# Two graph-attention layers on one core: the second layer's aggregates 1 to 4 split once more by Strassen

## The chip, the cores and the metric

The kernel runs on one core of a Trainium2 chip. Its engines are TensorE (matrix products, with a separate stream of weight loads), VectorE and ScalarE (elementwise work, and the only readers of PSUM, where TensorE writes), GpSimd (elementwise work in SBUF; it also issues the stores) and SyncE, which issues the loads. The metric is the device time of the program in microseconds, as the median of several runs.

## The reference, cut to what matters

There are 2708 nodes with 1024 features and an adjacency matrix of zeros and ones. Each of the two layers is a residual: x plus a graph attention of relu(layernorm(x)).

```python
# layer 0
h = relu(layernorm(x))
scores = where(adj > 0, relu((h @ Wf + bf) @ (h @ Wg + bg).T), NEG)
x = x + softmax(scores, axis=1) @ (h @ W + bW)
# layer 1
h = relu(layernorm(x))
hw = h @ W1
scores = where(adj > 0, leaky_relu(hw @ a1 + (hw @ a2).T), NEG)
x = x + relu(softmax(scores, axis=1) @ hw)
```

The kernel computes attention @ (h @ W) as (attention @ h) @ W. In layer 1 the scores need only two numbers per node, and the large products are attention @ h, called the aggregate, and the one with W, called the projection. All of it is float32.

## The kernel before, in words

**Tiling.** The 2708 rows are cut into 20 full tiles of 128 rows, one tile of 128 more (`MONO`) and one of 20 (`TINY`). The columns of the attention matrix, which are the output rows, are cut into five panels of 576, 576, 532, 512 and 512 (`width`, line 89). The full tiles go in ten pairs (`pairs`, line 109); ha and hb are the rows of a pair's two tiles.

**One Strassen level (Winograd's form, 7 products for 8).** An aggregate has three dimensions: the 1024 features, in two halves of 512 (4 column blocks of 128 each), the rows in pairs, where the two tiles of a pair are the two halves, and the panel's columns in two halves of width h. The left operand is made of the rows of h; its seven combinations M1 to M7 are stored in DRAM by `pair_h` (line 309; `rows_h` and `sums_h` in layer 0) and loaded again as `hc`. The right operand is made of the exponentials, called `P` in layer 1 (22 tiles per panel). `aggregate` (line 841) makes the right-hand sums T1, `second` and `fourth` and calls `accumulate` (line 603). There each of the seven half-wide products takes 10 pairs x 4 column blocks into four PSUM banks, in the order M1, M5, M2, M6, M3, M7, M4. The banks x, y, z and v are evicted by VectorE (ScalarE for M1 and M2). M6's banks go on to M7, M5's to M3, M1's to M2.

**Rows left over.** `MONO` and `TINY` don't take part in the splitting. `left_over` (line 877) adds them into the open banks of M2, M3 and M4, and into banks of its own in the middle of M7 (`into_m15`): one load `hl`, 8 instructions of 128 rows (line 883) and 8 of 20 rows that use a quarter of the array each (line 887).

**Scaling.** `inverse_sums` (line 814) makes the inverse sums of the softmax; the result gT is multiplied by them, mostly by GpSimd (`scale`, line 931), the last quarter by VectorE (line 939).

**What sets the order.** The Tile framework plans all instructions together by their place in the program and by its own estimates, so an engine may run one ahead of its place when its inputs are ready. Loads on SyncE's queue are pinned to program order by `load` (line 137). GpSimd's DMAs, stores and fetches alike, are not. Work for VectorE and ScalarE that has to fit between matmuls stands in a list, `later`, with an estimated time for each item. `behind(us)` (line 198) is called between groups of matmuls and issues items up to a credit:

```python
credit[0] = min(credit[0] + us, 2 * us)
while later and credit[0] > 0 and (psum_free or not later[0][3]) and (not later[0][4] or later[0][4]()):
    credit[0] -= one()
```

In the second layer's aggregates the rate is 4.0 after every third pair. The exponentials of the next panel are such items (`weights1`, line 1460, 24 items of 2.1 us). They are put in the list by a hook of `then`: `take_shifts` after M3 (it empties the list, takes column maxima with five transposes and makes the shifts) and `take_weights` after M7. `exps_until` (line 830) forces what isn't done when it is needed: half of the exponentials at the start of the aggregate, the rest after M5.

**Buffers.** There are 54 slots of 576 floats a partition (`slot`), 12 stream buffers of 1024 floats (`stream`; `hc`, `w` and the scores' operands are in these), two gT tiles and 8 PSUM banks.

**The scores loop of layer 0** (`scores`, line 1115) has already a form that the change takes over: for each pair, seven small products with accumulators X, Y and Z, in the order M1 X, M6 Z, M5 Y, M2 X, M7 Z, M3 Y and M4 Z. The last is delayed until after the next pair's first, so that VectorE has time to read Z.

Of the kernel before, what the change touches and what calls it, by code (L numbers as in the profile page):

```python
# [8 lines left out]
FP = mybir.dt.float32  # L9
# [48 lines left out]
def kernel(  # L58
# [69 lines left out]
    def stream(name, shape=(P, D), dt=FP):  # L128
        return strm.tile(list(shape), dt, tag="strm", name=name)
# [7 lines left out]
    def load(o, i):  # L137
        for a, b in in_16(o, i):
            tc.keep_in_program_order(nc.sync.dma_start(a, b))

    def store(o, i):
        for a, b in in_16(o, i):
            nc.gpsimd.dma_start(a, b)  # L143
# [10 lines left out]
    groups = [[q, q + 1] for q in range(0, NQ, 2)]  # L154
    group_of = {q: (i, j) for i, g in enumerate(groups) for j, q in enumerate(g)}
    assert sorted(group_of) == list(range(NQ))
    hg_d = [[dram.tile([P, 7, len(g), W], FP, name=f"hg{l}_d{i}") for i, g in enumerate(groups)] for l in range(2)]
    hsl_d = dram.tile([P, 2, NH, P], FP, name="hsl_d")
    hgl_d = [dram.tile([P, 2, W + P], FP, name=f"hgl{l}_d") for l in range(2)]
    md_d = dram.tile([P, 7, NH, W], FP, name="md_d")  # L160
    wt_d = [dram.tile([P, 4, NH, W], FP, name=f"wt{l}_d") for l in range(2)]
    mk_d = [dram.tile([P, NQ + 1, 2, width[p]], BF, name=f"mk_d{p}") for p in range(NP)]
# [17 lines left out]
        (nc.vector.tensor_copy if flip[0] else nc.scalar.copy)(o, i)  # L180


    later, credit = [], [0.0]
    ahead = [5]

    def put(us, go, fetch=None, takes_psum=False, ready=None):
        later.append([us, fetch, go, takes_psum, ready])

    def one():
        for it in later[:ahead[0]]:  # L190
            if it[1]:
                it[1]()
                it[1] = None
        us, _, go = later.pop(0)[:3]
        go()
        return us

    def behind(us, psum_free=False):
        credit[0] = min(credit[0] + us, 2 * us)
        while later and credit[0] > 0 and (psum_free or not later[0][3]) and (not later[0][4] or later[0][4]()):  # L200
            credit[0] -= one()

    def flush():
        while later:
# [96 lines left out]
    def left_h(l, hm, ht):  # L301

        for e in range(2):
            store(hgl_d[l][:, e, :W], hm[e])
            for d in range(NH):
                g = slice(B32 * d, B32 * (d + 1))
                store(hgl_d[l][g, e, W:], ht[e][g, d * P:(d + 1) * P])

    def pair_h(l, q, ha, hb):

        n = P
        on = nc.vector
        if q >= NQ - F // 2:
            s1, s2, s3, s4 = (slot(f"g{i}")[:, :W] for i in range(4))
            i, j = group_of[q]
            for m, h in ((M1, ha[0]), (M2, hb[0]), (M4, hb[1])):
                store(hg_d[l][i][:n, m, j], h)
            on.tensor_tensor(s1, ha[1], hb[1], OP.add)
            on.tensor_tensor(s2, s1, ha[0], OP.subtract)
            for m, h in ((M5, s1), (M6, s2)):  # L320
                store(hg_d[l][i][:n, m, j], h)

            def rest():
                on.tensor_tensor(s4, hb[0], s2, OP.subtract)
                on.tensor_tensor(s3, ha[0], ha[1], OP.subtract)
                for m, h in ((M3, s4), (M7, s3)):
                    store(hg_d[l][i][:n, m, j], h)
            return rest
        g1, g2 = stream("g1", (P, 2, W)), stream("g2", (P, 2, W))
        s1, s2, s3, s4 = g1[:n, 0], g1[:n, 1], g2[:n, 0], g2[:n, 1]  # L330
        on.tensor_tensor(s1, ha[1], hb[1], OP.add)
        on.tensor_tensor(s2, s1, ha[0], OP.subtract)
        on.tensor_tensor(s3, ha[0], ha[1], OP.subtract)
        on.tensor_tensor(s4, hb[0], s2, OP.subtract)
        i, j = group_of[q]
        for m, h in ((M1, ha[0]), (M2, hb[0]), (M4, hb[1])):
            store(hg_d[l][i][:n, m, j], h)
        store(hg_d[l][i][:n, M5:M6 + 1, j], g1[:n])
        store(hg_d[l][i][:n, M7:M3 + 1, j], g2[:n])

    def rows_h(q, ha, hb):

        i, j = group_of[q]
        for m, h in ((M1, ha[0]), (M5, ha[1]), (M2, hb[0]), (M4, hb[1])):
            store(hg_d[0][i][:, m, j], h)

    summed = [0]

    def sums_h():

        def fetch(q, two):
            i, j = group_of[q]
            for m in (M1, M2):
                two.append(stream("hr", (P, 2, W)))
                load(two[-1], hg_d[0][i][:, m:m + 2, j])

        def first(q, two):
            (a0, a1), (b0, b1) = ((t[:, 0], t[:, 1]) for t in two)
            add(b1, a1, b1)
            sub(a1, a0, a1)  # L360

        def second(q, two):
            (a0, a1), (b0, b1) = ((t[:, 0], t[:, 1]) for t in two)
            sub(a0, b1, a0)
            sub(b0, b0, a0)
            i, j = group_of[q]
            store(hg_d[0][i][:, M6:M7 + 1, j], two[0])
            store(hg_d[0][i][:, M3, j], b0)
            store(hg_d[0][i][:, M5, j], b1)
            summed[0] += 1  # L370
        for q in range(NQ):
            two = []
            put(1.4, lambda q=q, two=two: first(q, two), lambda q=q, two=two: fetch(q, two))
            put(1.4, lambda q=q, two=two: second(q, two))

    u = consts.tile([P, NC], FP, name="u")
    v = consts.tile([P, NC], FP, name="v")
# [463 lines left out]
    def aggregate(l, p, S, sm, then={}, rate=3.0):  # L841
# [28 lines left out]
        def left(m, q, d):  # L870
            i, j = group_of[q]
            if (m, i) not in hc:
                hc[m, i] = stream("hc", (P, 2, W))
                load(hc[m, i], hg_d[l][i][:, m])
            return hc[m, i][:, j, d * P:(d + 1) * P]

        def left_over(ps, e, s, start=False):


            two = stream("hl", (P, W + P))  # L880
            load(two, hgl_d[l][:, e])
            for d in range(NH):
                nc.tensor.matmul(ps[d], two[:, d * P:(d + 1) * P], S[MONO][:, s], start=start, stop=False,
                                 skip_group_check=True)
            for d in range(NH):
                g = slice(B32 * d, B32 * d + NY)
                nc.tensor.matmul(ps[d], two[g, W:], S[TINY][g, s], start=False, stop=start, skip_group_check=True)

        def into_m15():
            ps = [bank(f"gw{d}")[:, :h] for d in range(NH)]  # L890
# [40 lines left out]
        def scale():  # L931
            for e, s, k in ((0, slice(0, w), w), (1, hi, h)):
# [4 lines left out]
                   by_k=True, more={M2: lambda ps: left_over(ps, 0, lo), M3: lambda ps: left_over(ps, 0, hi),  # L937
                                    M4: lambda ps: left_over(ps, 1, lo), (M7, NQ // 2): into_m15})
        nc.vector.tensor_tensor(of(1, lo), of(1, lo), by(lo, h), OP.mult)
        return [t.rearrange("p (c i) -> p c i", c=NH) for t in G]  # L940

    w_in = [w0, w1]
# [166 lines left out]
    def put_max(p, q):  # L1109
        for k in range(2):  # L1110
            mk = []
            put(0.7, lambda k=k, mk=mk: raise_max(p, q, k, mk[0][:, :width[p]]),
                lambda k=k, mk=mk: mk.append(load_mask(p, q, k)))
# [164 lines left out]
        nc.vector.scalar_tensor_tensor(c, f1, ALPHA, m, op0=OP.mult, op1=OP.subtract)  # L1278
        return z, c, m

    done_rows, first_mask, raise_later = {}, {}, []

    def rows_done(t, xt):

# [13 lines left out]
        if panel_of[t] == NP - 1:  # L1298
            done_rows[t] = row_halves("h_last")
            normalize(xt, done_rows[t])  # L1300
            if whole and q == NQ - 1:
                tc.keep_in_program_order(nc.scalar.activation(stats.tile([P, 1], FP, name="warm"), eps, AF.Exp))
            raise_it = lambda: raise_max(0, q, k, first_mask[t][:, :width[0]])
            if not whole:
                dots(1)
                raise_later.append(raise_it)
                put(1.6, lambda: dots(0))
            else:
                raise_later.pop()()
                dots(1)  # L1310
                raise_it()
                put(1.6, lambda: dots(0))
                rest = []
                make = lambda: rest.append(pair_h(1, q, *(done_rows[s] for s in pairs[q])))
                if q == NQ - 1:
                    got["zm"] = shifts1(0, make)
                else:
                    make()
                rest[0]()
                for p in range(1, NP):  # L1320
                    put_max(p, q)
            return

        def met():
# [8 lines left out]
        if whole and q == LEFT:  # L1333
            put(0.0, lambda: left_h(1, *(done_rows[s] for s in mine)))
            put(0.0, met)
        elif whole:
            put(2.7, lambda: pair_h(1, q, *(done_rows[s] for s in pairs[q])))
            put(0.0, met)

    def halves_of_tiny(name):  # L1340
        t = slot(name)[:, :2 * P].rearrange("p (e j) -> p e j", e=2)
# [194 lines left out]
    def take_shifts(p):  # L1536
        flush()
        got["zm"] = shifts1(p)
# [5 lines left out]
    for p in range(NP):  # L1544
        S, sm = got["P"]
        then = {}
        if p + 1 < NP:
            then = {M3: lambda p=p: take_shifts(p + 1), M7: lambda p=p: take_weights(p + 1)}
        g = aggregate(1, p, S, sm, then, rate=4.0)
        project(1, p, g, finish1(p), by_pair=(p == NP - 1), rate=1.7)  # L1550


# [27 lines left out]
```

## Time and profile before

| | |
|---|---|
| median of 3 runs | 3132.92 us (3130.36 to 3140.10) |
| profiled execution: span, first to last instruction | 3135.8 us |
| profiled execution: time outside the span | not given by the page |
| TensorE matmul busy | 3053.1 us, 97% |
| weight loads busy | 2266.1 us, 72% |
| VectorE busy | 1835.6 us, 59% |
| ScalarE and GpSimd busy | 450.3 us and 427.3 us, 14% each |
| DMA | 666.04 MB, mean 212 GB/s |
| mean granted TensorE clock | 0.989 |

The second layer's aggregates start at 2157.27 us (panel 0), 2357.07, 2569.05, 2760.31 and 2941.69, and the projection follows each. The aggregates of panels 1 to 4 take 150, 138, 133 and 132 us. The profile comes as a page and as answers of the trace. A row of the timeline has a start in us, a duration, the engine, the line of the kernel, the operation, what it writes and reads, the shape and how many. A row of groups has the busy time and the mean duration in ns, then the engine's idle time before them and what ended it. Line 45 is that of a helper which issues every operation of VectorE and ScalarE, so these are told apart by their tiles. An f32 matmul of the program is two MATMUL instructions with two weight loads: the 40 matmuls of a half-wide product stand as x80.

### The profile page before, as it was taken

How to read it: one execution, taken by the hardware profiler on the slowest of the kernel's cores; microseconds unless marked ns; L12 is line 12 of the kernel's file. 1: busy time of each engine (PE TensorE's matmuls, PEld its weight loads, DVE VectorE, ACT ScalarE, POOL GpSimd, SP SyncE). 2: the span in 40 equal slices, each digit the busy share in tenths (PEclk: the TensorE clock that was granted, in tenths of full speed). 3: DMA queues.
4: the chain of work that ended last, by engine and by line, in shares of the span. 5: the costliest groups of instructions: out<-in, count | busy, mean ns of one | idle time of the engine just before them, and what ended most of it. 6: DMA issues, size and time to landing. Idle time of an engine off the chain costs nothing.

```text
span 3135.8 us, 36310 instructions
## 1 busy us (share of the span) xinstructions
PE 3053.1 (97%) x12694; PEld 2266.1 (72%) x12694; DVE 1835.6 (59%) x3767; ACT 450.3 (14%) x785; POOL 427.3 (14%) x654
## 2 busy tenths in 40 slices
PE   8998999899999999999999999998999999999998
PEld 4576777657877588886888885875757758678684
DVE  5766693776741686426973377758573571745612
ACT  3420020010200101101020002103131130311200
POOL 1421101310002110023000101021010020120202
PEclk9999999999999999999999999998999999999999
DMA  6989967988546796468955678597655565565655
GB/s 220 294 252 248 292 247 253 301 275 230 175 136 156 222 247 223 149 153 253 284 180 160 171 214 245 191 293 250 200 179 175 158 200 158 171 197 172 219 169 181
DMA packets 386278, 666.04 MB, mean 212 GB/s; under 512 B 171744, under 2 KB 212224, under 8 KB 386096
## 3 DMA queue, kind: packets, MB, share of 16 engines
q1 hardware_dynamic: 341936, 536.96, 56.9%
q0 software_dynamic: 44160, 126.76, 12.6%
q8 instruction: 101, 1.65, 0.2%
q14 instruction: 81, 0.66, 0.1%
HBM read 548.26 MB, written 115.30 MB: 212 GB/s over the span
## 4 chain that ended last, share of the span: by engine, by line
PE 81%; issue 6%; DVE 6%; DMA 5%; SPq 1%; POOL 1%; ACT 0%; POOLq 0%; DVEq 0%; ACTq 0%
PE gz L617 11%; PE gx L617 11%; PE gy L617 10%; PE sz L1140 6%; PE pz L1029 5%; PE gv L617 5%; PE sx L1140 4%; PE sy L1140 4%; PE px L1029 4%; PE py L1029 4%; PE M_ps L530 3%; PE qz L617 2%; PE qx L617 2%; PE qy L617 2%; DVE junk L45 1%
## 5 line engine op out<-in xcount | busy, mean ns | idle before, releaser
L1140 PE MATMUL sz<-B,As 128*128 128x288 f32 (+2 forms) x1200 | 295.9, 396 | 12.1 <-DVE st L45 7.9
L1140 PEld LDWEIGHTS sz<-B,As 128*128 128x128 f32 x1200 | 229.4, 192 | 63.1 <-DVE st L45 11.8
L933 POOL TENSOR_TENSOR gT<-gT,rr 128x2304 f32<-128x2304 f32 (+5 forms) x20 | 73.0, 3648 | 1081.4 <-DVE rr L45 979.3
L1140 PE MATMUL sx<-B,As 128*128 128x288 f32 (+2 forms) x800 | 201.5, 395 | 11.2 <-DMA As<-hs_d 9.1
L1140 PE MATMUL sy<-B,As 128*128 128x288 f32 (+2 forms) x800 | 199.3, 392 | 0.0
L617 PE MATMUL gz<-Sa,hc 128*128 128x288 f32 (+2 forms) x800 | 190.3, 399 | 5.9 <-DMA hc<-hg_d 5.9
L617 PE MATMUL gx<-P,hc 128*128 128x288 f32 (+2 forms) x800 | 187.0, 394 | 0.1
L617 PE MATMUL gz<-P,hc 128*128 128x288 f32 (+2 forms) x800 | 185.5, 392 | 0.0
L1140 PEld LDWEIGHTS sx<-B,As 128*128 128x128 f32 x800 | 152.5, 191 | 45.2 <-DMA As<-hs_d 10.1
L617 PE MATMUL gy<-T,hc 128*128 128x288 f32 (+2 forms) x800 | 184.2, 391 | 0.0
L617 PEld LDWEIGHTS gz<-Sa,hc 128*128 128x128 f32 x800 | 154.6, 194 | 40.0 <-DMA hc<-hg_d 6.4
L617 PEld LDWEIGHTS gx<-P,hc 128*128 128x128 f32 x800 | 152.4, 191 | 34.2 <-issue 3.7
L1140 PEld LDWEIGHTS sy<-B,As 128*128 128x128 f32 x800 | 152.3, 191 | 30.8
L617 PEld LDWEIGHTS gz<-P,hc 128*128 128x128 f32 x800 | 151.3, 190 | 31.6 <-issue 1.8
L617 PEld LDWEIGHTS gy<-T,hc 128*128 128x128 f32 x800 | 152.0, 190 | 30.5
L1029 PE MATMUL pz<-w,ps 128*128 128x512 f32 x320 | 142.1, 594 | 0.8 <-DVE pt L45 0.8
L1029 PE MATMUL py<-w,ps 128*128 128x512 f32 x320 | 141.9, 593 | 0.0
L1029 PE MATMUL px<-w,gT 128*128 128x512 f32 x320 | 141.0, 593 | 0.0
L143 POOL DMA_DIRECT2D out_dram<-x_res x180 | 89.2, 502 | 269.7 <-DVE x_res L45 264.5
L1029 PEld LDWEIGHTS pz<-w,ps 128*128 128x128 f32 x320 | 60.2, 190 | 77.1 <-issue 71.0
L1029 PEld LDWEIGHTS py<-w,ps 128*128 128x128 f32 x320 | 60.6, 190 | 75.5 <-issue 73.1
L530 PE MATMUL M_ps<-wgT,wfT 128*128 128x512 f32 x256 | 112.9, 597 | 1.6 <-ACT hsT L45 1.6
(319 smaller groups left out, 4894.9 us busy)
## 6 DMA issues: line engine op xcount, KB each, us to landing
hc<-hg_d SPq DMA_DIRECT2D x350, 512.0 KB, 3.7
As<-hs_d SPq DMA_DIRECT2D x150, 512.0 KB, 5.2
w<-wt_d SPq DMA_DIRECT2D x96, 512.0 KB, 4.9
w<-in_L_gnn_W_dram SPq DMA_DIRECT2D x72, 512.0 KB, 4.8
md<-md_d SPq DMA_DIRECT2D x56, 512.0 KB, 5.7
adj_i<-in_adj_dram SPq DMA_DIRECT2D x200, 128.0 KB, 5.2
hs_d<-hsT POOLq DMA_DIRECT2D x40, 512.0 KB, 7.2
As<-hs_d SPq DMA_DIRECT2D x50, 256.0 KB, 4.8
```

The costliest lines, as they stand in the source:

```text
L45: i = f(*a, **k)
L143: nc.gpsimd.dma_start(a, b)
L530: nc.tensor.matmul(ps, wfT[a][c // NH][:, c % NH, :], wgT[b][c], start=(c == 0), stop=(c == NC - 1))
L617: nc.tensor.matmul(ps[d], left(m, k, d), right(m, k), start=(start and k == 0), stop=(k == K - 1), skip_group_check=True)
L933: nc.gpsimd.tensor_tensor(of(e, s), of(e, s), by(s, k), OP.mult)
L1029: nc.tensor.matmul(ps, left[i][m][:, k, :], w_[k], start=(start and k == 0), stop=(k == NH - 1), skip_group_check=True)
L1140: nc.tensor.matmul(ps[:n, :h], lefts[q][:, i % 2, c, :n], B[m][c // 2][:, c % 2, :h], start=(start and c == 0), stop=(c == NH - 1), skip_g ...
```

## The change

Layer 0 and the second layer's panel 0 keep one level of Strassen. In panels 1 to 4, M1 and M5 stay half-wide, and each of M2, M6, M7, M3 and M4 (`BY_QUARTERS`) is split once more into seven small products. The second level takes as halves: the two pairs of a group of four tiles (5 groups, `NK`), two of the four column blocks, and a half of h (`hb`: 144, 133, 128 and 128 columns). A small product is then 5 groups x 2 column blocks, and lies in one PSUM bank.

- The left combinations of the layer's rows are all in one DRAM tile `hr_d`, in 1 KB pieces, ordered so that the groups of four tiles are neighbours. Of each split product, four more combinations per group are made by `put_quarters`: a fetch by GpSimd's queue, four adds of 256 columns, a store to `hs2_d`. These 25 items stand in a second list `lazy`, which `behind` serves when `later` is empty; `quarters_until` forces the rest.
- The right combinations (`quarter_sums`) are four subtractions of `hb` columns a group, 20 for each split product, issued during the product before.
- A split product loads nine stream buffers: one of four groups for each small product, and two that hold the fifth group for all of them.
- The results of the small products are added together in `V` and then into gT's quarters (`into_place`). The left-over rows go into the open banks X, Y, Z and a fourth, U; those of the (1,1) quarter go into four banks of their own (`corner`).
- In panels 1 to 3 `take_shifts` follows M7 and `take_weights` follows M3, as the order of products is now M1, M5, M2, M6, M7, M3, M4. The rate between small products is 1.2.

```diff
+    hr_d = dram.tile([P, 7, 2, 2, NK, WH], FP, name="hr_d")
+    hs2_d = dram.tile([P, 7, 4, NK, WH], FP, name="hs2_d")
...
-            store(hg_d[l][i][:n, m, j], h)
-        store(hg_d[l][i][:n, M5:M6 + 1, j], g1[:n])
+            store(rows_at(m, q), as_blocks(h))
+        store(rows_at(slice(M5, M6 + 1), q), as_blocks(g1[:n]))
...
+        while not later and lazy and credit[0] > 0:
+            credit[0] -= one(lazy)
...
+    BY_QUARTERS = (M2, M6, M7, M3, M4)
+    def put_quarters(m, k):
+        two = []
+        def fetch():
+            two.append(stream("hq", (P, 4, WH)))
+            nc.gpsimd.dma_start(two[0], hr_d[:, m, :, :, k].rearrange("p h f c -> p (h f) c"))
+        def go():
+            a11, a12, a21, a22 = (two[0][:, i] for i in range(4))
+            add(a22, a21, a22)
+            sub(a21, a11, a21)
+            sub(a11, a22, a11)
+            sub(a12, a12, a11)
+            store(hs2_d[:, m, :, k], two[0])
+            made_quarters[m] = made_quarters.get(m, 0) + 1
+        put(1.7, go, fetch, to=lazy)
...
+    def aggregate_quartered(p, S, sm, then={}, rate=3.0, fine=1.2):
...
+        def quarter_sums(m):
+            for k in range(NK):
+                r11, r12, r21, r22 = (part_of(m, k, i) for i in ((0, 0), (0, 1), (1, 0), (1, 1)))
+                four = slot("quarter", (P, 4, WX // 4))
+                t = {n: four[:, i, :hb] for i, n in enumerate((M5, M6, M7, M4))}
+                sub(t[M5], r12, r11)
+                sub(t[M6], r22, t[M5])
+                sub(t[M7], r22, r12)
+                sub(t[M4], r21, t[M6])
+                sums[m, k] = t
...
+        def product(m, n, ps, start):
+            quarters_until(m)
+            if (m, 0) not in lasts:
+                for i, of in enumerate((hr_d[:, m, :, :, NK - 1].rearrange("p h f c -> p (h f) c"), hs2_d[:, m, :, NK - 1])):
+                    lasts[m, i] = stream("hl2", (P, 4, WH))
+                    load(lasts[m, i], of)
+            t = stream("hc2", (P, NK - 1, WH))
...
+            load(t, hr_d[:, m, i // 2, i % 2, :NK - 1] if raw else hs2_d[:, m, i, :NK - 1])
+            last = lasts[m, int(not raw)][:, i]
+            for k in range(NK):
+                for d in range(2):
+                    lhs = t[:, k] if k < NK - 1 else last
+                    nc.tensor.matmul(ps[:, d], lhs[:, d * P:(d + 1) * P], inner_right(m, n, k),
+                                     start=(start and k == 0 and d == 0), stop=(k == NK - 1), skip_group_check=True)
+            behind(fine)
...
+        accumulate(left, operand, NQ, h, (M1, M5), then,
+                   {M1: first_product, M5: lambda d, ps: add(quad(0, hi)[:, d], ps, quad(0, lo)[:, d])}, "g",
+                   {M5: second}, rate=rate, by_k=True, more={(M5, NQ // 2): first_sums})
...
+        place = {M2: [(0, lo)], M6: [(0, hi), (1, lo)], M7: [(1, hi), (1, lo)], M3: [(0, hi)], M4: [(1, lo)]}
...
+        before_next = {M2: lambda: (fourth(), quarter_sums(M6)), M6: lambda: quarter_sums(M7),
+                       M7: lambda: quarter_sums(M3), M3: lambda: quarter_sums(M4)}
+        left_out = None
+        for m in BY_QUARTERS:
+            V = in_pairs("V")
...
+            X = bank2("gx")
+            product(m, M1, X, True)
+            nc.scalar.copy(c21, X)
+            if left_out:
+                left_out()
+            Z = bank2("gz")
+            product(m, M6, Z, True)
+            add(c12, Z, c21)
+            Y = bank2("gy")
+            product(m, M5, Y, True)
+            add(c22, Y, c21)
+            if m == M7:
+                corner()
+            if m in before_next:
+                before_next[m]()
+            product(m, M2, X, False)
+            if m not in more_of:
+                nc.scalar.copy(c11, X)
+            product(m, M7, Z, False)
+            add(c22, Z, c22)
+            product(m, M3, Y, False)
+            if m in more_of:
+                U = bank2("gu")
+                left_over({(0, 0): X, (0, 1): Y, (1, 0): Z, (1, 1): U}, *more_of[m], [(1, 1)])
+                nc.scalar.copy(c11, X)
+            add(c12, Y, c12)
+            if m in more_of:
+                add(c22, U, c22)
+            into_place(m, V, 0)
+
+            def left_out(m=m, V=V, Z=Z, c21=c21):
+                product(m, M4, Z, False)
+                add(c21, Z, c21)
+                into_place(m, V, 1)
+                if m == M3:
+                    scale()
...
-            then = {M3: lambda p=p: take_shifts(p + 1), M7: lambda p=p: take_weights(p + 1)}
-        g = aggregate(1, p, S, sm, then, rate=4.0)
+            then = dict(zip((M7, M3) if p else (M3, M7), (lambda p=p: take_shifts(p + 1), lambda p=p: take_weights(p + 1))))
+        g = aggregate_quartered(p, S, sm, then, rate=4.0) if p else aggregate(1, p, S, sm, then, rate=4.0)
```

## The prediction

> **What bounds the kernel now.** I read four things in order: the page's busy table, the chain that ended last, the engines by stage in the second layer, and TensorE's timeline inside one aggregate.
>
> The page's table of busy time, and its chain (shares of the span):
>
> ```profile
> PE 3053.1 (97%) x12694; PEld 2266.1 (72%) x12694; DVE 1835.6 (59%) x3767; ACT 450.3 (14%) x785; POOL 427.3 (14%) x654
> ...
> PE 81%; issue 6%; DVE 6%; DMA 5%; SPq 1%; POOL 1%; ACT 0%; POOLq 0%; DVEq 0%; ACTq 0%
> ```
>
> TensorE works nearly all the time and the chain is TensorE's. Busy time by stretch (us, then PE, PEld, DVE, ACT, POOL, clock, DMA share, GB/s), over panel 1's aggregate, and over three stretches of panel 0's:
>
> ```profile
> 2357.00:2507.00 150.00, 150.00 (x643) 115.53 (x642) 63.44 (x122) 20.98 (x38) 11.60 (x10) 1.00 0.53 162
> ```
> ```profile
> 2220.00:2239.00 19.00, 19.00 (x80) 14.89 (x79) 5.57 (x12) 0.37 (x1) 0.00 (x0) 1.00 0.45 129
> 2239.00:2262.00 23.00, 23.00 (x101) 17.56 (x100) 2.23 (x5) 0.00 (x0) 0.00 (x0) 1.00 0.61 186
> 2262.00:2286.00 24.00, 24.00 (x110) 18.27 (x109) 14.50 (x28) 0.42 (x2) 5.10 (x2) 1.00 0.46 144
> ```
>
> In the aggregates that change, TensorE is never idle, VectorE is idle for over half, and DMA moves 162 GB/s. So a matmul cycle saved here shortens the end, as long as the other engines keep up. The chain in order of time gives one half-wide product (80 instructions: 10 pairs of row tiles x 4 column blocks, each f32 matmul being two instructions) in panels 1, 2 and 3; panel 4 equals 3:
>
> ```profile
> 2376.63 19.40 PE gy L617 x80
> ...
> 2587.15 17.93 PE gy L617 x80
> ...
> 2777.74 17.27 PE gy L617 x80
> ```
>
> Per instruction that is 242.5, 224.1 and 215.9 ns for 288, 266 and 256 columns: 0.833 ns a column plus about 2.5 ns.
>
> **What the Trainium skill says.** (1) "TensorE: Matmul & The Clock Gate", Part 1, section "Wait — 56ns, not 53.3ns?": warm matmuls start N/2.4 GHz + about 2.5 ns apart. The trace agrees on the constant; f32 costs two cycles a column, in each of the two instructions. The same section says that without hardware decoding the sequencer spends about 62 ns a matmul; the slow loads and matmuls here can't show that. (2) The same page, Part 2, "Step-by-step: what each phase is for": the next tile's weights load while this one's matmul runs. The trace agrees (below). (3) "DMA: Bandwidth & Descriptors", Specifications: full rate from 512 B a piece, fabric 435 GB/s. The trace reached 405 GB/s over 40 us.
>
> **The change, part by part.** *Matmuls.* A split product has 7 small products x 5 k x 2 column blocks x 2 instructions = 140 of half the width, for 80 of the whole. At 144, 133 and 128 columns the fit gives 122.5, 113.3 and 109.2 ns. What the trace of before lacks is a 128-column f32 matmul with its own full weight load, whose record lasts 190 ns. Ends: 109.2 (load hidden) and 190 (loads never overlap). TensorE's matmuls, then its loads, near 62 us:
>
> ```profile
> 62.52 1.91 PE L399 MATMUL h_ps<-ident,x 128*128 128x128 f32 x16
> 64.26 1.02 PE L530 MATMUL M_ps<-wgT,wfT 128*128 128x512 f32 x2
> ```
> ```profile
> 62.41 1.78 PEld L399 LDWEIGHTS h_ps<-ident,x 128*128 128x128 f32 x16
> 64.16 0.30 PEld L530 LDWEIGHTS M_ps<-wgT,wfT 128*128 128x128 f32 x2
> ```
>
> Sixteen 128-column transposes start (64.26 - 62.52)/16 = 109 ns apart, and two full loads of 190 ns together take 300 ns, so they overlap by 80: load starts can be 110 ns apart. I take 112 ns at 128 columns. Per product: 140 x 122.5 = 17.15 for 19.40 us (saves 2.25); 140 x 113.3 = 15.86 for 17.93 (2.07); 140 x 112 = 15.68 for 17.27 (1.59). Five products a panel: 11.25 + 10.35 + 7.95 + 7.95 = **-37.5 us** (-41.5 at 109.2).
>
> *Left-over rows.* Now, from TensorE's timeline:
>
> ```profile
> 2411.39 2.10 PE L883 MATMUL gx<-P,hl 128*128 128x288 f32 x8
> 2413.42 0.77 PE L887 MATMUL gx<-P,hl 20*128 20x288 f32 x8
> 2414.12 4.15 PE L617 MATMUL gx<-P,hc 128*128 128x288 f32 x16
> ```
>
> A call takes 2414.12 - 2411.39 = 2.73 us, 0.70 of it the tiny rows. After: 16 x 122.5 = 1.96, and the tiny ones are 16 in four concurrent groups instead of 8 in two: between 0.70 and 1.40, taken as 1.0. So +0.25 a call, 16 calls: **+4.0 us** (0 to +12).
>
> *VectorE.* Adds cost (mean ns):
>
> ```profile
> L45 DVE TENSOR_TENSOR P<-P 128x288 f32<-128x288 f32 x40 | 16.9, 448 | 17.6 <-PE gx L617 17.6
> L45 DVE TENSOR_TENSOR P<-P 128x256 f32<-128x256 f32 x40 | 15.8, 418 | 31.0 <-PE gx L617 31.0
> ```
>
> with 686 for 512 columns, so about 285 at 128. Added a panel: 100 quarter sums (28.5 us), 28 inner evictions (11.7), 14 placings of 512 (9.6), corner 4 (1.7); removed: 24 evictions (10.0). Net +41 us, on 63.4 of 150 in panel 1: 105 of about 142. It hides behind TensorE; uncovered it would cost all 41 a panel. ScalarE's 10 more copies of 0.4 us are hidden likewise. What can show is a late operand: each small product accumulates into a bank that VectorE or ScalarE must first have read, and behind a waiting matmul stands all of TensorE, so the next bank comes late too. The scores loop already works like this (X, Z, Y, X, Z, Y, Z, last product delayed):
>
> ```profile
> PE sz L1140 <- DVE st L45: 7.9, 7, 2.0
> ...
> PE sx L1140 <- DVE sm L45: 2.1, 3, 1.3
> ```
>
> With 1.0 more on its r, 11 us over 50 x 7 products: 0.031 each. For 140 products **+4.4 us** (0 to +20, 1 us an outer product).
>
> *Start of a panel.* Exponentials begin after M3, which is again one product before the end, but that product is shorter by 4 us at most and VectorE has about 8 us more in it. They then run on into the next panel's M5, where VectorE is idle 17 of 19 us, and meet the 6 us of M2's sums there. M2 waits if they are late: **+3 us** over three panels (0 to +15). The swapped hooks (five transposes, short VectorE steps, spreads, 22 mask loads on SP) stay behind the fifth and sixth of seven products: 0; the one such spread that was not covered cost 3.9 us.
>
> *Sums of the left operand.* 25 groups of 4 adds of 256: 41.8 us of VectorE, 26 MB of DMA, 50 issues on POOL of about 0.54 us. Those of the first three panels fall into layer 0's aggregates and score operands, the rest into panel 0's last products, where VectorE is idle 66 - 22.3 = 43.7 us. POOL's fetches can wait for a stream buffer, with its stores and the scaling of gT queued behind; the first scaling has a product's worth of cover. **+2 us** (-2, the planner's order shifting, to +10). Uncovered it would be 41.8.
>
> *DMA and SP.* 9 loads of 512 KB for 5: 4.72 MB in about 16.5 us, 286 GB/s. SP issues 9 x 0.32 = 2.9 us; mask loads stand in the same order. Twelve stream buffers less the held last pair give some 8 small products of lead, 17 us, against 3.7 us to landing. Such a rate was seen at the end of the first layer (columns as above):
>
> ```profile
> 2100.00:2140.00 40.00, 38.81 (x90) 16.63 (x88) 26.09 (x55) 5.64 (x10) 7.79 (x15) 1.00 1.04 405
> ```
>
> So 0. Stores in 1 KB pieces: as many issues, 0.
>
> **Sum:** -37.5 + 4.0 + 4.4 + 3 + 2 = -24.1 us. From the profiled span of 3135.8: 3111.7; what lies around that span the page doesn't give, and I take it as unchanged. The median of the runs, 3132.92, lies 2.9 lower: **3109 us**. A third of a per cent (9 us) is about what a measurement of this kernel can tell from no change.
>
> **Rivals.**
> *A, gain eaten.* TensorE's sequencer is the limit at short matmuls: 2 x 62 = 124 ns a pair, an estimate from the skill's section under (1). Then a product takes 17.36 us in every panel: saves 10.2 + 2.9 - 0.5 - 0.5 = 12; with +13.4 of the other terms: 3134. For it: no run of over 33 short pairs in the trace. Against it: those run at 109 ns. The same end follows if late starts cost 1 us an outer product. 0.10.
> *B, slower: VectorE late for the banks.* Four places in each of 20 split products accumulate into a bank just read by VectorE: 80 places. With 24 us net gain, the sign turns at 24/80 = 0.3 us a place beyond what I charged. The sums for the next product (5.7 us, with the 4.2 us of the fourth step before M6) are written ahead of the eviction of M7's small product; if VectorE does them in that order at every product and TensorE waits 0.8 us a place, +64: 3173. For it: the sums are as long as two and a half small products. Against it: operands are ready early and VectorE was idle there. 0.17.
> *C, slower: DMA.* If 1 KB pieces and mask loads hold the rate to 220 GB/s, a split product takes 4.72/0.22 = 21.5 us, +5 each, 100 in all: 3209. It decides below some 270 GB/s. Against: 405 above. 0.05.
> *D, slower: weight loads at 190 ns*, 26.6 us a product: about +190. The overlapping pair speaks against it. 0.03.
> The products are counted from the code, so that the change does less than it says is not a case of its own.
>
> **How the numbers follow.** Forecast 0.65, its own range 3091 to 3123; A 0.10; B, C, D 0.25. Faster 0.65, same 0.10, slower 0.25. The low end is -41.5 with nothing lost and the planner's -2: 3090. The high end takes in A and B's lower half, 3160, and leaves out B's upper half, C and D, about 0.16.
>
> **What would show it.** Right: split products of 15.3 to 15.8 us (128 columns) and 17.2 (144), small matmuls 109 to 123 ns apart; TensorE idle by a few us in aggregates 1 to 4; VectorE 65 to 80% busy there; about 290 GB/s. Wrong: a pace near 124 at all widths (A); TensorE waiting on VectorE or ScalarE at gx, gy or gz, or on slots (B); on hc2 (C); a pace of 190 (D); or a longer first layer.

## The result and the profile after

The changed kernel takes **3144.74 us** (median of 4 runs, 3140.32 to 3146.53), the kernel before 3131.64 us (3128.17 to 3140.10). The ratio is **1.0037**, with a 95% interval of 1.0018 to 1.0056: slower by about 0.4%, a small difference, but the interval lies wholly above 1. The profiled spans are 3144.8 and 3135.8 us. The forecast was 3109, with a range of 3090 to 3160.

First the page of the changed kernel, busy time and chain:

```profile
PE 3026.1 (96%) x14150; PEld 2298.4 (73%) x14150; DVE 2013.0 (64%) x4355; ACT 462.5 (15%) x825; POOL 473.9 (15%) x704
...
PE 76%; DMA 8%; DVE 7%; issue 6%; SPq 2%; POOL 1%; ACT 1%; POOLq 0%; DVEq 0%; ACTq 0%
```

TensorE works 27 us less, and yet the span is longer. In the chain, TensorE's share fell from 81 to 76% and DMA's rose from 5 to 8%.

The table gives the length of the stages that changed, from TensorE's first instruction in each to its first in the next (us; every other stage between panel 0's projection in layer 0 and the last projection of layer 1 differs by at most 0.2):

| stage | before | after | difference |
|---|---|---|---|
| start to the scores of panel 1 | 667.2 | 659.0 | -8.2 |
| layer 0, scores of panel 1 | 151.9 | 161.4 | +9.5 |
| layer 0, scores of panel 2 | 138.7 | 150.1 | +11.5 |
| layer 0, scores of panel 3 | 137.7 | 151.2 | +13.5 |
| layer 0, last projection | 67.0 | 80.1 | +13.1 |
| layer 1, aggregate of panel 0 | 151.7 | 152.0 | +0.3 |
| layer 1, aggregates of panels 1 to 4 | 553.9 | 524.3 | -29.6 |

The aggregates that were changed won 29.6 us. **Layer 0, whose products weren't changed, lost 47.6 us** in four stages.

The aggregate of panel 1 (busy time by stretch, columns as before):

```profile
2397.00:2539.00 142.00, 139.57 (x1008) 128.92 (x1008) 93.64 (x235) 19.44 (x40) 11.94 (x10) 1.00 0.75 237
```

142 us instead of 150, VectorE at 66%, DMA at 237 GB/s; TensorE is still busy 98% of the time. TensorE's timeline in panel 1 (left-over rows) and panel 3 (two small products):

```profile
2450.33 0.65 PE L1062 MATMUL gx<-P,hl 128*128 128x144 f32 x4
...
2453.08 2.23 PE L1047 MATMUL gx<-P,hc 128*128 128x144 f32 x16
...
2818.52 1.95 PE L1047 MATMUL gx<-P,hc 128*128 128x128 f32 x16
2820.30 0.61 PE L1047 MATMUL gx<-P,hl 128*128 128x128 f32 x4
2820.75 1.95 PE L1047 MATMUL gz<-quarter,hc 128*128 128x128 f32 x16
```

A small product is 20 instructions: (2820.75 - 2818.52)/20 = 111.5 ns at 128 columns, where the forecast had 112. A left-over call takes 2453.08 - 2450.33 = 2.75 us, 0.02 more than before. What TensorE waited for, longest in total (us in total, times, longest):

```profile
PE sx L1365 <- DMA As<-hs_d: 32.9, 6, 9.6
PE px L1254 <- DMA w<-in_L_gnn_W_dram: 10.9, 1, 10.9
...
PE gy L1047 <- DVE V L45: 4.1, 3, 1.8
```

In the split products TensorE waits 4.1 us for VectorE at gy and 2.1 us more at gz. The long waits are elsewhere: for As, the left operand of the *scores*, and for w in layer 0's last projection (before: none). Of the 32.9 us for As, 12.7 lie in the scores of panel 0, where the kernel before has all its 9.1 us of this wait; the other four waits, 20.2 us, lie in panels 1 to 3, where it has none.

What stands in front of such a wait? The chain in order of time, inside panel 1's scores:

```profile
690.02 4.08 DMA hr_d<-g
...
694.15 9.99 DMA adj_i<-in_adj_dram
...
704.21 5.25 DMA As<-hs_d
...
709.50 4.21 PE sx L1365 x8
```

Five sums of the left operand (`put_quarters`) are served just there: their fetches are issued at 692, 693, 695, 695 and 711 us, their stores from 703 on, 5 x 1 MB in all. SyncE has to wait for the store of `g` to free a stream buffer; then the loads of the adjacency matrix crawl (9.99 us to landing, where this load's median on the page is 5.3), and As, which stands behind them in SyncE's order, is issued only when one of them has landed, at 704.21. TensorE stands for 6.4 us and then does 8 matmul instructions in 4.21 us, which elsewhere in this loop take 2.10, and the next 16 in 4.9 instead of 4.0: its granted clock is 0.73 from 710 to 720 us. The 6.4 us of waiting and 3.0 of slow matmuls make up the 9.5 us of this stage.

The Trainium skill, "TensorE: Matmul & The Clock Gate", section "What's actually happening", says that the array falls to half its clock after an idle window of about 3.4 us. The trace agrees on the half pace, which follows the wait of 6.4 us. It doesn't agree that the wait itself has to last 3.4 us: waits of 1.1 to 1.8 us at gy and one of 1.85 us at sx bring no slow matmuls, but one of 2.16 us in the same scores does (8 instructions in 3.03 us, where 2.10 is usual; the kernel before has the like after 1.98 us). In the kernel with the layout only, below, the same wait of 2.16 us brings none, so its length alone doesn't decide.

```profile
683.35 3.03 PE L1365 MATMUL sz<-B,As 128*128 128x288 f32 x8 [2.16 <-DVE st L45]
```

Not all of the 47.6 us belongs to the sums. In panel 3 their fetches begin at 1556 us, but TensorE is already 5.2 us behind the kernel before well ahead of them. It waits there for VectorE, which waits, by way of ScalarE, for a DMA of rows of x, and the matmuls after it are slow. After, then before:

```profile
1480.85 3.78 PE L1365 MATMUL sx<-B,As 128*128 128x256 f32 x8 [3.79 <-DVE sm L45]
```
```profile
1465.52 1.99 PE L1140 MATMUL sx<-B,As 128*128 128x256 f32 x8 [1.26 <-DVE sm L45]
```

Why this wait is longer here stays open. It leaves at most 8.3 us of panel 3's 13.5, and some 42 us of the four stages, to the sums.

### The profile page after: what moved, and what is told of

Same layout as the page of the kernel before. It is cut to its first block, busy times and chain, and to the rows that moved or that the text cites. A ratio compares the mean times of both kernels' runs of the same rounds, so it can differ in the third digit from the quotient of the medians.

```text
span 3144.8 us, 40235 instructions
## 1 busy us (share of the span) xinstructions
PE 3026.1 (96%) x14150; PEld 2298.4 (73%) x14150; DVE 2013.0 (64%) x4355; ACT 462.5 (15%) x825; POOL 473.9 (15%) x704
## 4 chain that ended last, share of the span: by engine, by line
PE 76%; DMA 8%; DVE 7%; issue 6%; SPq 2%; POOL 1%; ACT 1%; POOLq 0%; DVEq 0%; ACTq 0%
PE gx L654 8%; PE gy L654 8%; PE sz L1365 6%; PE gz L654 5%; PE pz L1254 5%; PE sx L1365 4%; PE px L1254 4%; PE py L1254 4%; PE gz L1047 4%; PE sy L1365 4%; PE M_ps L567 3%; PE qz L654 3%; PE gx L1047 3%; PE gy L1047 2%; PE gv L654 2%
## 5 line engine op out<-in xcount | busy, mean ns | idle before, releaser
L1365 PEld LDWEIGHTS sz<-B,As 128*128 128x128 f32 x1200 | 229.4, 192 | 59.0 <-DVE st L45 12.2
L1365 PE MATMUL sx<-B,As 128*128 128x288 f32 (+2 forms) x800 | 210.4, 408 | 37.2 <-DMA As<-hs_d 32.9
L1365 PEld LDWEIGHTS sy<-B,As 128*128 128x128 f32 x800 | 152.4, 191 | 32.0 <-DVE st L45 1.3
L654 PEld LDWEIGHTS gy<-T,hc 128*128 128x128 f32 x800 | 152.0, 190 | 30.5
L970 POOL TENSOR_TENSOR gT<-gT,rr 128x2304 f32<-128x2304 f32 (+5 forms) x12 | 44.4, 3700 | 569.3 <-DVE rr L45 529.1
L1254 PEld LDWEIGHTS px<-w,gT 128*128 128x128 f32 x320 | 60.9, 193 | 83.5 <-issue 81.5
L1047 PE MATMUL gz<-quarter,hc 128*128 128x128 f32 (+2 forms) x960 | 120.4, 279 | 0.0
L1047 PEld LDWEIGHTS gz<-quarter,hc 128*128 128x128 f32 x960 | 114.7, 191 | 0.5
L654 PE MATMUL gx<-P,hc 128*128 128x288 f32 (+2 forms) x480 | 113.7, 398 | 0.1
```

Source lines behind the costliest of these rows:

```text
L654: nc.tensor.matmul(ps[d], left(m, k, d), right(m, k), start=(start and k == 0), stop=(k == K - 1), skip_group_check=True)
L970: nc.gpsimd.tensor_tensor(of(e, s), of(e, s), by(s, k), OP.mult)
L1047: nc.tensor.matmul(ps[:, d], lhs[:, d * P:(d + 1) * P], inner_right(m, n, k), start=(start and k == 0 and d == 0), stop=(k == NK - 1), ski ...
L1254: nc.tensor.matmul(ps, left[i][m][:, k, :], w_[k], start=(start and k == 0), stop=(k == NH - 1), skip_group_check=True)
L1365: nc.tensor.matmul(ps[:n, :h], lefts[q][:, i % 2, c, :n], B[m][c // 2][:, c % 2, :h], start=(start and c == 0), stop=(c == NH - 1), skip_g ...
```

## The experiments

Two theories at the start. **P, the place**: the sums of the left operand, served in layer 0, hold up the loads of As and w. **L, the layout**: the left operand now goes to DRAM in 1 KB pieces, and these stores are what lengthens layer 0. Each run's ratio is to the kernel before on the same chip. The table collects the stages that tell (us):

| kernel | scores 1 | scores 2 | scores 3 | last projection of layer 0 | layer 1 panel 0 | panels 1 to 4 |
|---|---|---|---|---|---|---|
| before | 151.9 | 138.7 | 137.7 | 67.0 | 151.7 | 553.9 |
| changed | 161.4 | 150.1 | 151.2 | 80.1 | 152.0 | 524.3 |
| layout only | 151.8 | 138.7 | 137.9 | 67.0 | 152.4 | 553.9 |
| sums unused | 161.3 | 149.3 | 144.8 | 83.4 | 152.3 | 553.9 |
| sums late | 151.9 | 138.7 | 138.8 | 67.0 | 194.9 | 524.4 |
| late, traffic in the old places | 161.4 | 146.4 | 138.9 | 81.6 | 192.6 | 524.4 |
| late, additions in the old places | 154.2 | 138.7 | 140.2 | 66.9 | 192.4 | 524.4 |
| own buffers | 161.3 | 150.8 | 146.3 | 75.4 | 151.6 | 524.3 |
| late, own buffers | 149.6 | 138.7 | 137.6 | 66.9 | 198.8 | 524.4 |
| spread over aggregates | 152.8 | 138.7 | 138.8 | 67.3 | 151.8 | 525.2 |
| spread in the scores | 151.7 | 139.9 | 141.7 | 67.0 | 152.7 | 524.4 |
| spread, late | 149.5 | 138.6 | 137.6 | 66.9 | 188.4 | 525.2 |

### 1. Layout alone, and sums that nobody reads

```diff
-        g = aggregate_quartered(p, S, sm, then, rate=4.0) if p else aggregate(1, p, S, sm, then, rate=4.0)
+        g = aggregate(1, p, S, sm, then, rate=4.0)
```

This leaves the sums in place and reads none. With a `return` at the head of `put_quarters` as well, only the layout remains.

> The new layout of the left operand (hr_d, 1 KB pieces, wider left-over rows), no sums at all, panels 1 to 4 by one level. Theory P: as before within 4 us, 3128 to 3136. Rival L: 3165 to 3175.

> Layout and sums as in the changed kernel, in the same places, but panels 1 to 4 are computed by one level of Strassen as before, so the sums are made and never read. Theory P: the kernel before plus 40 us, 3168 to 3178. If layer 1's gain was only apparent, or the loss comes from the split products: 3132 to 3140.

Layout only: 3125.74 us, ratio 0.9978 (0.9969 to 0.9986), just below the range that P gave. Sums unused: 3174.00 us, ratio 1.0129 (1.0111 to 1.0147). L is dead: the layout costs nothing. (It is a little faster than before, nearly all of it ahead of the scores of panel 1, where layer 1's operands aren't made yet; most kernels tried here arrive there 3 to 15 us sooner than the one before. I have no explanation for that part beyond a changed order of work.) The sums cost 48 us between these two kernels, 43 of it in the four stages, without a single split product. So the changed kernel is two things: a gain of some 29 us in layer 1, and a loss of some 48 in layer 0.

### 2. The sums kept back until layer 1

```diff
-        put(1.7, go, fetch, to=lazy)
+        put(1.7, go, fetch, to=late)
...
-        while not later and lazy and credit[0] > 0:
-            credit[0] -= one(lazy)
+        while not later and second[0] and late and credit[0] > 0:
+            credit[0] -= one(late)
```

`second[0]` is set when layer 1's panel 0 begins.

> All 25 sums of the left operand are kept back until layer 1's panel 0; layer 0 makes none. Theory P (the place of these sums: inside the scores of layer 0, and just before its last projection, they hold up the loads of As and w, some 40 us): layer 0 as long as before within 3 us, layer 1 shorter by about 30, time 3101 to 3110 us. Rival L (the new layout, whose stores go out in 1 KB pieces, is what lengthens layer 0): layer 0 stays some 40 us longer, time about 3144. A third possibility: 25 sums in one panel are too many, and panel 0 or the first split product of panel 1 gets longer by up to 20 us.

3139.08 us, ratio 1.0024 (1.0015 to 1.0034). P's time was missed, though its place was right: layer 0 is as before, but panel 0 of layer 1 has become 43.2 us longer. The possibility named third was the one, and twice as bad as I had allowed. The loss moves with the sums. Stretches of panel 0 in this kernel, and VectorE's longest wait there:

```profile
2260.00:2280.00 20.00, 13.98 (x52) 9.42 (x50) 8.51 (x21) 0.00 (x0) 8.22 (x11) 0.83 0.96 325
2280.00:2300.00 20.00, 0.00 (x0) 0.00 (x0) 8.83 (x22) 0.00 (x0) 6.09 (x9) 0.55 0.95 325
```
```profile
DVE hq L45 <- DMA hq<-hr_d: 37.7, 14, 6.2
```

TensorE does nothing for 20 us while VectorE is busy less than half. VectorE stands at sums whose fetch hasn't landed, 14 times, and the evictions of gy, which TensorE needs next, are behind these sums in VectorE's order. DMA is full from 2240 to 2320 us (share 0.95 to 1.03).

### 3. Traffic or additions?

On the kernel with late sums, dummies were served in layer 0 in the old places: only fetch and store, or only the four additions. In the second text P-B and P-R are two forms of P-D: that buffers are held (B), or the traffic itself (R).

```diff
+        def fetch0():
+            held.append(stream("hz", (P, 4, WH)))
+            nc.gpsimd.dma_start(held[0], hr_d[:, m, :, :, k].rearrange("p h f c -> p (h f) c"))
+
+        def go0():
+            store(hz_d[:, m, :, k], held[0])
+        put(1.7, go0, fetch0, to=lazy)
```

> The sums kept back as in the first of these kernels, and in their old places in layer 0 only the traffic of 20 to 25 of them: a fetch of 512 KB into a buffer of the stream pool and a store of it to a scratch array that nobody reads, no additions. Theory P-D (buffers and DMA traffic are what costs): 30 us or more over the kernel with the sums kept back, 3133 to 3148. Theory P-V (the four additions in VectorE's fixed order are what costs): within 6 us of it, 3103 to 3112.

> As the kernel with the sums kept back until layer 1, and in their old places in layer 0 only the additions: four of 256 columns for each of the 20 to 25 sums, on a constant tile, without fetch, store or stream buffer. P-B and P-R: within 5 us of the kernel with the sums kept back, 3134 to 3145. If VectorE's fixed order in the scores is what costs: 3160 to 3180.

Traffic: 3172.44 us, ratio 1.0131 (1.0113 to 1.0150), 33 us over late sums as P-D had it (its times were too low, as they were built on late sums of some 3103 us). Additions: 3140.34 us, ratio 1.0038 (1.0025 to 1.0051), some 4 us over them by the ratios. So it is mainly the traffic, not the additions in VectorE's fixed order: fetch and store alone bring +9.5, +7.7 and +14.6 us back in the scores of panels 1 and 2 and in the last projection. In panel 3 they bring nothing, where the whole sums cost up to 8.3; additions bring 1.4 there and 2.3 in panel 1. Panel 3 isn't settled by these two runs.

### 4. Held buffers or the traffic itself?

SyncE's loads wait for stream buffers, and each sum holds one of the twelve until its store has landed. If that is what costs (P-B), buffers of their own end it; if it is the traffic (P-R), they don't.

```diff
-            two.append(stream("hq", (P, 4, WH)))
-            nc.gpsimd.dma_start(two[0], hr_d[:, m, :, :, k].rearrange("p h f c -> p (h f) c"))
+            for h in range(2):
+                two.append(slot("hq", (P, 2, WH)))
+                nc.gpsimd.dma_start(two[h], hr_d[:, m, h, :, k])
```

> As the changed kernel, in the same places, but each sum of the left operand is fetched into two tiles of the slots pool (256 KB each) instead of one of the twelve stream buffers, with two fetches and two stores for one. Theory P-B (what costs is that loads of As, hc and w wait in SP's order for a stream buffer that a sum holds until its store has landed): the waits of SP on the store of hq are gone, scores of panels 1 to 3 within 4 us of the kernel before, time 3098 to 3112. Theory P-R (the added traffic itself, in stages where DMA is busy nine tenths already): scores still 8 to 13 us longer each, time 3135 to 3150.

> As the kernel with the sums kept back until layer 1's panel 0 (which got 43 us longer), but with the fetched halves in tiles of the slots pool instead of stream buffers. Theory P-B (there the loads of hc wait for a stream buffer until a sum's store has landed): panel 0 within 10 us of before, 3100 to 3112. Theory P-R (26 MB more in one panel are more than DMA gives): panel 0 still 30 to 45 us longer, 3128 to 3145.

In the old places: 3135.83 us, ratio 1.0024 (1.0016 to 1.0033). Late: 3141.59 us, ratio 1.0027 (1.0016 to 1.0039). P-R's times came out in both (panel 0 of the late kernel is 47.1 us longer, a little more than P-R's 30 to 45). In the old places the scores are still 9.4, 12.2 and 8.6 us longer. In panel 1 the wait for As is gone, and another has come in its place (two views of that stage, what TensorE and what VectorE waited for):

```profile
PE sz L1367 <- DVE st L45: 7.4, 3, 4.5
```
```profile
DVE hq L45 <- DMA hq<-hr_d: 6.9, 4, 2.7
```

With a free buffer, As is loaded in time, but then the sums' own fetches are late, VectorE stands at them in its fixed order, and TensorE behind VectorE. Only the last projection clearly gained, 4.7 us of its 13.1: there the buffers have a part. (In panel 3 the long wait at the start is absent from this kernel; its 8.6 us stand against the 8.3.)

### 5. The same traffic, spread

One sum at a time, in the aggregates alone, counted in calls:

```diff
+    calls, EVERY = [None], 4
+
+    def calm():
+        if calls[0] is None:
+            return
+        i = calls[0] % EVERY
+        if i == 0 and lazy and lazy[0][1]:
+            lazy[0][1]()
+            lazy[0][1] = None
+        if i == 2 and lazy and not lazy[0][1]:
+            lazy.pop(0)[2]()
+        calls[0] += 1
```

`calm` is called after each `behind` of `accumulate`; `calls[0]` is set to 0 ahead of layer 0's aggregates 1 to 4 and of layer 1's panel 0.

> As the changed kernel, but the sums are served one at a time, one in every four calls inside the aggregates alone (layer 0's panels 1 to 4 and layer 1's panel 0, some 20 us apart), none in the scores or in the projections. Both P-B and P-R expect layer 0 within 4 us of the kernel before and the gain of layer 1 kept: 3094 to 3106. If the sums cost their time wherever they stand (the sum of left operands is never free), it stays at 3135 to 3145.

**3097.60 us, ratio 0.9907 (0.9895 to 0.9919)**: faster than both kernels. The fetches are now mostly 14 to 27 us apart, in the aggregates or just ahead of them; from panel 0's projection on each stage of layer 0 is as before within 1.1 us, panel 0 of layer 1 too, and 28.7 us of gain stay in panels 1 to 4. (The scores of panel 1 also begin 7.6 us sooner, much as with the layout alone.)

Is it that the scores have no room at all, or that five at once are too many?

```diff
+        every[0], calls[0] = 12, 0 if 1 <= p <= 3 else None
         got["S"], got["acc"] = scores(p, B)
+        every[0], calls[0] = 4, None
```

> As the kernel with the sums spread over the aggregates, but those of the first three panels are served inside the scores of panels 1 to 3 of layer 0 again, one at a time, some 29 us apart, instead of five in a row. Theory bunch (five sums at once, 5 MB within some 20 us, are more than DMA has left there): each of the scores at most 3 us longer than before, 3098 to 3107. Theory total (those stages have no room for 5 MB at all): each 8 to 12 us longer, 3120 to 3133.

3105.83 us, ratio 0.9917 (0.9904 to 0.9931). The scores are -0.2, +1.2 and +4.0 us off: crowding, mostly. Panel 3 is just past the 3 us that theory bunch allowed, which may be the amount. The DMA share, next to last column, shows the difference. First the changed kernel, then this one, then one stretch of the kernel before:

```profile
700.00:710.00 10.00, 3.56 (x14) 2.58 (x13) 9.58 (x23) 0.00 (x0) 2.07 (x3) 0.92 1.08 308
710.00:720.00 10.00, 10.00 (x32) 7.34 (x32) 4.11 (x9) 0.00 (x0) 1.50 (x2) 0.73 1.05 313
720.00:740.00 20.00, 20.00 (x84) 15.70 (x83) 14.39 (x34) 0.00 (x0) 2.83 (x4) 1.00 0.99 293
```
```profile
700.00:710.00 10.00, 10.00 (x43) 7.85 (x42) 8.83 (x21) 0.00 (x0) 1.30 (x2) 1.00 1.07 270
710.00:720.00 10.00, 10.00 (x43) 7.85 (x42) 6.30 (x14) 0.00 (x0) 1.31 (x2) 1.00 0.95 219
720.00:740.00 20.00, 20.00 (x85) 15.64 (x84) 14.11 (x31) 0.00 (x0) 1.31 (x2) 1.00 0.88 260
```
```profile
710.00:720.00 10.00, 10.00 (x43) 7.85 (x42) 7.08 (x15) 0.00 (x0) 0.56 (x1) 1.00 1.00 263
```

A full stretch of 20 us is met by loads issued ahead, and the kernel before has such stretches too. With five sums DMA stays full from 690 to 740 us, and the lead of As runs out.

Then all 25 in panel 0, one at each call of its aggregate:

> As the changed kernel, but all 25 sums stand in the aggregate of layer 1's panel 0, one at each of its 28 calls (some 5.4 us apart, each fetched two calls ahead), none in layer 0. That panel moves 176 GB/s x 152 us = 26.8 MB by itself; 25 x 1.05 = 26.2 MB come on top, 349 GB/s over the whole panel. Theory rate (what counts is what DMA can move in the stretch; 325 to 353 GB/s were seen there at full share): panel 0 longer by 3 to 15 us instead of 43, 3098 to 3112. Theory bunch alone (only the crowding counts, not the amount): within 3 us of before, 3093 to 3100. If a sum's fetch holds up VectorE wherever it stands: 30 us or more, 3125 to 3140.

3136.40 us, ratio 1.0012 (1.0004 to 1.0019): theories rate and bunch are both missed, as panel 0 is still 36.7 us longer. The time is in the range of the third theory, that a sum's fetch holds up VectorE wherever it stands; but the kernel with the spread sums, where the same fetches cost next to nothing, speaks against that. The sums were spread in the program, not in time:

```profile
2170.00:2190.00 20.00, 20.00 (x84) 15.68 (x83) 20.00 (x37) 10.48 (x18) 3.54 (x5) 1.00 0.38 117
2190.00:2210.00 20.00, 10.99 (x37) 8.07 (x36) 20.00 (x47) 4.19 (x7) 6.96 (x10) 0.74 1.02 342
```

VectorE is busy without a gap here, so the first sums wait for their turn with their buffers held, and from 2170 to 2190 DMA works at little over a third (0.38). From 2190 to 2290 it is full, at 342 to 380 GB/s. A mean over the panel, with which I had worked, says nothing about that. Whether 25 sums would fit into this panel if they were really even stays untested.

### 6. Fetch or store?

On the spread kernel, in the old places, only a fetch into slots, or only a store from a constant tile:

```diff
+        def go0():
+            store(hz_d[:, m, :, k], wab[0].rearrange("p (i c) -> p i c", i=4))
```

> As the kernel with the sums spread over the aggregates, and in the old places of layer 0, five in a row, only a fetch of 512 KB each again (into slots, nobody reads it), no addition, no store. If reading and writing weigh alike: half of the 31 us by which these stages are longer in the kernel with fetch and store only, so 3108 to 3118. If the stores in 1 KB pieces are what costs: 3096 to 3103.

> The same, with only a store of 512 KB for each sum in the old places (from a constant tile, to an array that nobody reads; so no stream buffer is held), no fetch, no addition. If reading and writing weigh alike: 3108 to 3118. If the stores in 1 KB pieces are what costs: 3120 to 3135. If it is the wait of stream buffers for the stores' landing, which is absent here: 3096 to 3103.

Fetches: 3114.41 us, ratio 0.9942 (0.9928 to 0.9956), and nearly all of the loss is one stage: the last projection, +12.6, with waits for w of 6.0 and 1.9 us; in the scores at most +1.6. Stores: 3128.24 us, ratio 0.9982 (0.9972 to 0.9993), but this run didn't test what it was made for. A store of a constant depends on nothing, so the planner moved all twenty ahead, to 610 to 640 us, into the projection of panel 0, which grew from 48.1 to 73.7 us by one wait:

```profile
PE py L1279 <- DMA w<-wt_d: 23.3, 1, 23.3
```

It is crowding again, in pure form: 20 x 512 KB = 10.5 MB of stores within 30 us, no addition and no buffer held by a sum, DMA at a share of 1.03 to 1.06 from 610 to 640 us, and w comes 23 us late. The share alone doesn't tell this: in the kernel before it is as high there (1.11, 1.01 and 1.03), with no such wait. Whether the scores suffer more from the fetches or from the stores stays open; the fetches alone aren't enough.

## Why the prediction was wrong

**The step that failed is "Sums of the left operand": +2 us (-2 to +10), where these sums cost some 42 of the 47.6 us that the four stages lost.** (That this is near the 41.8 us named for uncovered additions is chance: additions alone cost some 4 us.) Three things in it were wrong. *Where they run*: I let those of the first three panels "fall into layer 0's aggregates and score operands"; `behind` serves them wherever the list `later` is empty, and that was inside the scores of panels 1, 2 and 3, five in a row, and at the end of layer 0's last aggregate. *What they use*: I asked whether VectorE had time, and named its 41.8 us as the price if uncovered. The 26 MB I counted and then weighed against nothing. In the kernel before the scores of panel 1 have a DMA share of 0.81 at 235 GB/s, and those of panel 3 have 0.91; I had looked at the aggregates' 0.53. *What is late next*: I had fetches wait for a buffer, not loads wait for the fetches' traffic.

**DMA and SP, "So 0"**, held where I worked it out: the split products never wait for a left operand, at a share of 0.75 to 0.84. It was taken for the whole kernel without looking at the other stages. And the 405 GB/s that I quoted as proof of room is no ceiling for all loads: in the scores DMA is full at 270 to 313 GB/s. (The 0 for stores in 1 KB pieces held: the layout alone cost nothing.) The skill's page "Perfetto Trace Analysis", section "Identifying the Most-Contended Engine", advises to judge DMA by the use of the memory's bandwidth rather than by the busy share. Here neither was enough: at 313 GB/s and a share of 1.05 loads were late, at 263 GB/s and 1.00, or 405 GB/s and 1.04, in the kernel before they were not.

**The terms of layer 1** were right in sum: -26.1 forecast (-37.5 + 4.0 + 4.4 + 3), -29.3 measured with panel 0. *Matmuls*: 111.5 ns for 112 at 128 columns, 122.5 for 122.5 at 144; seven small products in a row took 3026.07 - 3010.34 = 15.73 us in panel 4 by the timeline, where 15.68 was forecast. *Left-over rows*: +0.02 a call instead of +0.25, so about 0 instead of +4.0; sixteen tiny ones in four groups take 0.70 us, as eight in two did. *Late operands and start of a panel*: 7.4 forecast, and TensorE's waits on VectorE in these aggregates add up to 6.2 us; but that is luck. The waits weren't spread over the products or at the start of a panel: they are six, all in the last 11 us of the aggregates of panels 1 to 3.

**The rivals.** A's sequencer limit of 124 ns is refuted by 111.5. B, VectorE late for the banks, cost under 2.5 us a panel, not 16. C looked for the slow DMA in the split products, where it wasn't; the mechanism was the right one in the wrong stage. D is refuted: loads of 190 ns stay hidden at 111.5 ns a matmul. "Or a longer first layer" stood among the signs, with no price and no chance, and that is what came. The range up to 3160 took in the 3144.74 by luck: its upper part was made for A and B.

## What to carry to other kernels

Work that is hidden by compute still has to be placed where its resource is free, and a list that serves it "when there is time" knows only the time of the engine it was written for: look at DMA in the very stages where the items will run, and count fetch and store. Traffic for which there is room on average still stalls TensorE when it comes five items at once, because the next needed load comes late; one at a time, over layer 0's aggregates and one panel more, the same 25 items cost next to nothing and the change became a gain of 0.9%. And where a loss moves with the work from stage to stage, as with the late sums, look at how densely the work is served, not only at the place.

## What the runs showed of the hardware

Short f32 matmuls, each with a new full weight load of 190 ns, ran 111.5 to 112.4 ns apart, 140 in a row without a gap: the loads stay hidden down to 128 columns. A TensorE wait of 6.4 us costs 9.5, since the 24 matmul instructions after it take 3.0 us more. And 10.5 MB of stores issued within 30 us made a load that was needed next 23.3 us late.
